# Routed rows without filled slots: shorter routing chunks in layer 1, and layer 3's expert groups that write finished tokens

## The chip, the cores and the metric

The kernel runs on one core of a Trainium2 chip. The metric is the device time of the whole program in microseconds; lower is better. Two engines matter most below beside TensorE (PE): VectorE (DVE), which does the small arithmetic of the routing, and GpSimd (POOL), which issues the indirect DMAs. ScalarE (ACT) evaluates functions, and SyncE (SP) issues ordinary DMAs.

## The reference, cut to what matters

Four transformer layers run one after another on 8192 tokens of width 128, in float32. Each layer is an attention (or scan) followed by a feed-forward part. The change concerns the feed-forward parts of layers 1 and 3, which are mixtures of 8 experts.

```python
# layer 1 (top 2 of 8, hidden width 512)
logits = xf @ gate_w + gate_b
top_w, top_i = jax.lax.top_k(logits, K)                 # K = 2
gw = jax.nn.softmax(top_w, axis=-1)
combine = (gw[:, :, None] * one_hot(top_i, E)).sum(axis=1)
for e in range(E):
    h = gelu(xf @ w1[e] + b1[e])
    out = out + combine[:, e:e + 1] * (h @ w2[e] + b2[e])
shared = gelu(xf @ ws1 + bs1) @ ws2 + bs2
return out + shared

# layer 3 (one expert of 8: the best of 4 groups, then the better of its 2; hidden width 256)
x = layernorm(x + attn_out, ln1_g, ln1_b)
combine = one_hot(flat_e, E) * (g_prob * e_prob)[:, None]
moe = sum over e of combine[:, e] * (relu(x @ w1[e] + b1[e]) @ w2[e] + b2[e])
x = layernorm(x + moe, ln2_g, ln2_b)
```

Around every part stands a residual of the form `x = x + part(layernorm(x))`. So the last output is layer 3's input plus its second layernorm.

## The kernel before, in words

**Tokens.** The 8192 tokens stand as 64 tiles of 128 (NT = 64). The residual `K.x` stays in on-chip memory for the whole program.

**Slots.** Class `Slots` sorts tokens by expert through DRAM. `rows` has room for 8 experts, each with 8192+256 slots. A row is the token's 128 numbers, the place to which its result goes, and its weight. `fill` writes all 67584 slots of each layer in advance with blanks: zeros, and a place that lies behind the tokens and differs for each slot. It runs on POOL beside layer 0's feed-forward part: an `iota` (L333) for the places and a DMA (L337) of 390 KB, 88 times a layer.

**Routing.** A chunk of 16 tiles is routed at once. `settle` closes the norms of a chunk (DVE). `gate` turns tokens and computes logits (PE, ACT, DVE). `choose` picks the experts and their weights. `places` counts tokens per expert with matmuls and a scan, and gives every token its slot. Then `send` casts the 128 slots of a tile to integers (`one`, L1422, a ring of 8 tiles) and issues an indirect DMA on POOL that writes 128 rows to their slots (L478). Layer 1 has two copies of each token; between them `second` rewrites the place (L373) and weight (L1417) of the chunk's rows, and it has to wait for the first copies' sends. In layer 1 these are generators, and `beside(n, most)` advances each by n steps and issues up to `most` sends after each step of the attention or of the shared feed-forward part. The order of PE, ACT and DVE is written out by hand in this way, so an instruction that waits holds everything behind it on its engine.

**Layer 1.** 16 attention steps overlapped in stages (four tiles each) are followed by the shared feed-forward part. Its expert work starts when all rows are sent. `S.finish` works out, for every group of 256 slots, its expert and its first slot.

**Groups.** `experts` walks over groups of 256 slots (72 in layer 1, 40 in layer 3: as many as full groups would need, plus one for each expert). `fetch` reads `xs` (SP, L513), copies the expert's weights `w` (L520) and second bias `b2` (L522) on DVE, casts `place` (L524), transposes on PE (L527) and copies `xT` on DVE (L529). `rise` multiplies by the first weight (PE, L538) and applies the function (ACT, L544). `fall` multiplies by the second (PE, L552 and L557), multiplies by the weight (DVE `y`, L563) and issues two indirect DMAs that write 128 results each to `back` (POOL, L484). `xs` and `y` have four buffers.

**After the groups.** Layer 1's results are read back by the next stage. Layer 3's tail reads eight tiles at a time (`join`, L2639), adds them to the rows `y`, takes the statistics, normalizes (ACT, L2648), multiplies by gamma (DVE, L2655), adds the residual (POOL, L2656) and writes to the output with SP. In layer 3 the rows of all 64 tiles stay in one tile of on-chip memory (`row`), and the space also serves the stage between layers 2 and 3 (`middle`) as scratch. Layer 3's expert weights `w_all` are loaded by 16 DMAs and one for the bias on SP, when the attention has ended (L2618 to L2623).

Of the kernel before, what the change touches and what calls it, by code (L numbers as in the profile page):

```python
# [20 lines left out]
P = 128  # L21
# [203 lines left out]
class Norm:  # L225
# [18 lines left out]
    def take(self, src, lo, hi):  # L244
        for j in range(lo, hi):
            self.nc.vector.bn_stats(self.st[:, j, :], src[:, j, :])  # L246
# [57 lines left out]
class Slots:  # L304
# [8 lines left out]
    GROUP, WIDE, NE = 256, D + 2, 8  # L313
    ROOM = NT * P + GROUP

    def __init__(self, K, es, tag, ranks):
        self.K, self.tag, self.ranks = K, tag, ranks
        self.groups = ranks * NT * P // self.GROUP + self.NE
        self.count = self.NE * self.ROOM
        dram = K.pool(es, tag + "slots", 1, DRAM)  # L320
        self.rows = dram.tile([self.count, self.WIDE], F32, name=f"{tag}_rows")
        self.back = dram.tile([self.count + ranks * NT * P, D], F32, name=f"{tag}_back")

    def fill(self, pool):
        nc = self.K.nc
        n = 6
        blank = [pool.tile([P, n, self.WIDE], F32, name=f"blank{i}") for i in range(2)]
        for t in blank:
            nc.gpsimd.memset(t, 0.0)
        rows = self.rows.rearrange("(c p n) w -> c p n w", p=P, n=n)  # L330
        for i in range(self.count // P // n):
            t = blank[i % 2]
            nc.gpsimd.iota(  # L333
                t[:, :, D], pattern=[[1, n]], base=i * n * P, channel_multiplier=n,
                allow_small_or_imprecise_dtypes=True,
            )
            nc.gpsimd.dma_start(rows[i], t)  # L337

    def begin(self, pool, most):

        nc = self.K.nc
        self.every = pool.tile([P, P], BF16, name="every")
# [6 lines left out]
        self.go_on = pool.tile([P, self.NE, most], F32, name="go_on")  # L349
        nc.gpsimd.memset(self.go_on, 1.0)  # L350
        nc.gpsimd.memset(self.go_on[:, :, 0:1], 0.0)
# [19 lines left out]
    def belongs(self, row, j, n, rank):  # L371

        self.K.nc.gpsimd.iota(  # L373
            row[:, j : j + n, D], pattern=[[P, n]], base=self.count + (rank * NT + j) * P,
            channel_multiplier=1, allow_small_or_imprecise_dtypes=True,
        )

    def places(self, pool, bank, picks, out):
# [4 lines left out]
        n, most = picks[0].shape[1], self.go_on.shape[2]  # L383
# [23 lines left out]
        if n == most:  # L407
            nc.vector.tensor_tensor_scan(
                sums.rearrange("p e n -> p (e n)"), self.go_on.rearrange("p e n -> p (e n)"),
                total.rearrange("p e n -> p (e n)"), 0.0, ALU.mult, ALU.add,  # L410
            )
        else:
            for e in range(NE):
                nc.vector.tensor_tensor_scan(
                    sums[:, e, :], self.go_on[:, e, 0:n], total[:, e, :], 0.0, ALU.mult, ALU.add
                )
# [17 lines left out]
    def finish(self, pool, long, expert, start):  # L434
# [16 lines left out]
        past = pool.tile([1, n, NE - 1], F32, name="past")  # L451
        nc.vector.tensor_tensor(
            past, self.number.unsqueeze(2).to_broadcast([1, n, NE - 1]),
            end[0:1, 0 : NE - 1].unsqueeze(1).to_broadcast([1, n, NE - 1]), ALU.is_ge,
# [3 lines left out]
        nc.vector.tensor_scalar(expert, which, float(long), None, ALU.mult)  # L458
# [3 lines left out]
            past, past, need[0:1, 0 : NE - 1].unsqueeze(1).to_broadcast([1, n, NE - 1])  # L462
# [20 lines left out]
    def result(self, place, row):  # L483
        i = self.K.nc.gpsimd.indirect_dma_start(  # L484
            self.back, bass.IndirectOffsetOnAxis(ap=place, axis=0), row, None
        )
        self.free(self.tag + "result", i.ins)

    def experts(self, w_all, expert, start, F, act):
# [9 lines left out]
        with ExitStack() as ps:  # L499
            gp = K.pool(ps, tag + "g", 4)  # L500
            wp = K.pool(ps, tag + "gw", 3)
# [5 lines left out]
            def fetch(g):  # L507
# [4 lines left out]
                xs = gp.tile([P, N, self.WIDE], F32, name="xs")  # L512
                nc.sync.dma_start(  # L513
                    xs, self.rows[bass.ds(at, self.GROUP)].rearrange("(n p) w -> p n w", p=P)
                )
                at = nc.vector.value_load(
# [6 lines left out]
                place = gp.tile([P, N], mybir.dt.uint32, name="place")  # L523
                nc.vector.tensor_copy(place, xs[:, :, D])  # L524
# [4 lines left out]
                nc.vector.tensor_copy(xT, t)  # L529
# [19 lines left out]
            def fall(g):  # L549
# [12 lines left out]
                y = gp.tile([P, N, D], F32, name="y")  # L562
                nc.vector.tensor_mul(y, o, xs[:, :, D + 1 : D + 2].to_broadcast([P, N, D]))  # L563
                for i in range(N):
                    self.result(place[:, i : i + 1], y[:, i, :])

            with K.tc.manual_schedule(
                engines={nc.tensor.engine, nc.scalar.engine, nc.vector.engine, nc.sync.engine}
            ):
                for g in range(-1, self.groups + 1):  # L570
# [4 lines left out]
                    if g > 0:  # L575
                        fall(g - 1)

    def results(self, pool, n, eight):

        back = self.back[self.count :].rearrange("(r j p) d -> r p j d", r=self.ranks, p=P)  # L580
# [331 lines left out]
def l0_ffn(K):  # L912
# [4 lines left out]
    with ExitStack() as es:  # L917
# [44 lines left out]
        for slots in (K.slots1, K.slots3):  # L962
            slots.fill(sp)
# [289 lines left out]
def layer1(K):  # L1253
# [4 lines left out]
    FC, CHUNK = F // P, 16  # L1258
# [13 lines left out]
    with ExitStack() as es:  # L1272
# [16 lines left out]
        S.begin(sp, CHUNK)  # L1289
# [28 lines left out]
        def settle(lo):  # L1318
            hi = lo + CHUNK
# [15 lines left out]
        def gate():  # L1335
# [19 lines left out]
            if old is not None:  # L1355
                lo, at = 4 * old // CHUNK * CHUNK, 4 * old % CHUNK
                if at == 0:
                    logits[lo] = lw.tile([P, CHUNK, NE], F32, name="lg")
# [4 lines left out]
                if at == CHUNK - 4:  # L1363
                    active.append((choose(lo), lo))
# [4 lines left out]
        def choose(lo):  # L1369
            n, hi = CHUNK, lo + CHUNK  # L1370
            lg = logits.pop(lo)

            def new(name, *shape):
                return rw.tile([P, n, *shape], F32, name=name)
# [30 lines left out]
            yield from S.places(rw, lambda: hold.pop(lo), picks, slots)  # L1405
            sum_e = new("sum_e")
            nc.vector.tensor_scalar_add(sum_e, e, 1.0)
            yield
            w0 = row[:, lo:hi, D + 1]
# [5 lines left out]
            def second():  # L1415
                S.belongs(row, lo, n, 1)
# [8 lines left out]
            S.belongs(row, lo, n, 0)  # L1425
# [39 lines left out]
        with ExitStack() as at:  # L1465
# [79 lines left out]
            def third(blk):  # L1545
# [21 lines left out]
                if (4 * blk + 4) % CHUNK == 0:  # L1567
                    active.append((settle(4 * blk + 4 - CHUNK), None))

            with K.tc.manual_schedule(  # L1570
# [3 lines left out]
                for n in range(NBLK + 5):  # L1574
# [3 lines left out]
                    beside(10, 5)  # L1578
# [5 lines left out]
        with ExitStack() as ps:  # L1584
# [30 lines left out]
            with K.tc.manual_schedule(  # L1615
                engines={nc.tensor.engine, nc.scalar.engine, nc.vector.engine}
            ):
                for n in range(NBLK + 1):
# [4 lines left out]
                    beside(14, 4)  # L1623
# [5 lines left out]
        S.experts(w_all, expert, start, F, AF.Gelu)  # L1629
# [13 lines left out]
def attention(K, es, tag, rows, wq, wk, wv, qb, kb, wo, bias, dst, causal, beside, done, more):  # L1643
# [124 lines left out]
    def turn(b):  # L1768
# [7 lines left out]
        if bias is not None:  # L1776
            y = dst[:, 2 * b : 2 * b + 2, :]
# [171 lines left out]
    def join(b):  # L1949
# [8 lines left out]
        def add():  # L1958
            y = dst[:, 2 * b : 2 * b + 2, :]
# [71 lines left out]
def l2_attn(K):  # L2031
    nc, ins = K.nc, K.ins
    DC = 32
    with ExitStack() as es:
# [66 lines left out]
        for _ in attention(  # L2101
            K, es, "a2", rows, w[:, 0, :], w[:, 1, :], w[:, 2, :], None, None, wo, None, K.x, True,
            beside, done, more,
# [5 lines left out]
def middle(K, scratch, fills):  # L2109
# [6 lines left out]
    with ExitStack() as es:  # L2116
# [46 lines left out]

        def xT(blk):
            return scratch[:, blk * 512 : (blk + 1) * 512]
# [183 lines left out]
def l3_ffn(K):  # L2349
# [7 lines left out]
    with ExitStack() as es:  # L2357
        sp = K.pool(es, "f3", 1)
        row = sp.tile([P, NT, S.WIDE], F32, name="y")
        y = row[:, :, 0:D]  # L2360
# [12 lines left out]
        with ExitStack() as ps:  # L2373
# [46 lines left out]
            def rows(b):  # L2420
                while ready[0] < 2 * b + 2:
                    next(entering, None)
                for j in (2 * b, 2 * b + 1):
                    nc.scalar.activation(
                        y[:, j, :], K.x[:, j, :], AF.Identity, bias=nmr[:, j : j + 1],
                        scale=first.r[:, j : j + 1],
                    )
                return y[:, 2 * b : 2 * b + 2, :]
# [5 lines left out]
            def settle(lo):  # L2434
# [5 lines left out]
                for j in range(lo, hi, 2):  # L2440
                    two = y[:, j : j + 2, :]
# [10 lines left out]
            def gate(bank, late):  # L2452
# [8 lines left out]
                if new is not None:  # L2461
                    for i in range(2):
                        nc.tensor.transpose(t[:, i * P : (i + 1) * P], y[:, new + i, :], K.ident)
# [315 lines left out]
```

## Time and profile before

| what | value |
|---|---|
| median of 3 runs | 3095.63 us (3092.87 to 3099.08) |
| profiled execution | 3072.12 us, its span 3070.4 us |
| TensorE clock granted, mean | 0.906 |
| PE, DVE, ACT, POOL busy | 81%, 60%, 46%, 28% of the span |
| layer 0 | 0 to 833 us |
| layer 1: attention, shared part, end of sends, groups | 855 to about 1000, 991 to 1123.5, to 1202.7, to 1485 |
| layer 2 and the middle | 1520 to 2260 us |
| layer 3: attention, last sends and weights, groups, tail | 2260 to 2850, to 2876.9, to 2996, to 3070.4 |

The stages are read from the windows of the profile, counted from the start of the span. A busy share is an average over stages with different limits. A stage's limit is read from its own window: which engine is busy there, and which wait ends last.

### The profile page before, as it was taken

Reading aid. Unit: us, or ns where it says so; the run is one execution under the profiler, and the core shown is the slowest. Engines: PE = TensorE matmul, PEld = TensorE weight load, DVE = VectorE, ACT = ScalarE, POOL = GpSimd, SP = SyncE. Lnnn points to the kernel's source line nnn. Section 1 sums busy time; section 2 is a strip of 40 time slices with the busy share of each in tenths; the row PEclk is TensorE's granted clock in tenths of the full one; section 3 lists DMA queues with packets and bytes.
Section 4 is the critical chain, followed back from the end, with each engine's and each line's share of the span. In section 5 each row is a group of like instructions: output and inputs, shape, how many; then the busy total and the mean of one; then the engine's idle time right before and its main releaser. Section 6 shows DMA issues by size and latency. Waiting matters only on the chain.

```text
span 3070.4 us, 59293 instructions
## 1 busy us (share of the span) xinstructions
PE 2481.3 (81%) x21486; PEld 1840.0 (60%) x21486; DVE 1853.4 (60%) x5498; ACT 1426.3 (46%) x3065; POOL 853.9 (28%) x1235
## 2 busy tenths in 40 slices
PE   4899787899889962999488888996978888887470
PEld 4865444444857742999466667775855555555460
DVE  7215454444878312444379766764869988886447
ACT  3433432222468521444435555556427677776223
POOL 1001444310012455455310101100520223343573
PEclk9999789999989986999779989997979999999795
DMA  2497455540000211222455434430034445451334
GB/s 72 141 283 223 173 231 228 217 152 21 12 1 13 82 40 52 70 70 70 117 155 160 128 113 141 132 95 13 1 86 137 128 125 143 130 147 42 91 91 112
DMA packets 263264, 340.81 MB, mean 111 GB/s; under 512 B 34598, under 2 KB 231062, under 8 KB 254780
## 3 DMA queue, kind: packets, MB, share of 16 engines
q1 hardware_dynamic: 231228, 237.01, 27.1%
q0 software_dynamic: 27584, 97.92, 8.5%
q8 instruction: 170, 2.79, 0.4%
q10 hardware_dynamic: 4160, 2.10, 0.3%
q14 instruction: 122, 1.00, 0.1%
HBM read 156.72 MB, written 177.83 MB: 109 GB/s over the span
## 4 chain that ended last, share of the span: by engine, by line
PE 39%; DVE 12%; DMA 7%; issue 5%; ACT 5%; POOL 4%; SPq 1%; DVEq 0%; POOLq 0%; ACTq 0%
PE o L1909 5%; PE t L1888 5%; DVE top L1845 4%; PE o L557 4%; PE hp L538 4%; DMA q<-row 4%; PE s L1784 2%; PE s L1833 2%; POOL f_back L484 2%; PE d L1607 2%; PE a L1592 2%; ACT e L1896 2%; DMA f_rows<-row,one 2%; DVE st_x L246 1%; PE a L1492 1%
## 5 line engine op out<-in xcount | busy, mean ns | idle before, releaser
L1845 DVE TENSOR_REDUCE top<-s 128x3 f32<-128x384 f32 (+1 forms) x1024 | 600.5, 617 | 189.5 <-PE s L1742 133.3
L1896 ACT ACTIVATE e<-t 128x384 f32<-128x384 f32 (+1 forms) x1024 | 494.0, 546 | 128.2 <-PE s L1742 82.7
L1888 PE MATMUL t<-q,k 64*128 64x256 f32 (+1 forms) x2048 | 417.1, 308 | 115.8 <-ACT e L1896 60.9
L1833 PE MATMUL s<-k,q 48*128 48x256 f32 (+1 forms) x2048 | 437.8, 331 | 30.3 <-DMA k<-d 16.7
L1888 PEld LDWEIGHTS t<-q,k 64*128 64x128 f32 x2048 | 299.7, 191 | 194.8 <-ACT e L1896 90.2
L1833 PEld LDWEIGHTS s<-k,q 48*128 48x128 f32 x2048 | 308.2, 198 | 43.6 <-DVE top L1845 23.9
L544 ACT ACTIVATE h<-hp,w 128x256 f32<-128x256 f32 x368 | 154.6, 471 | 332.8 <-PE hp L538 324.0
L484 POOL DMA_INDIRECT f_back<-y,place x224 | 217.4, 970 | 191.8 <-DVE y L563 125.8
L1909 PE MATMUL o<-e,val 128*32 128x256 f32 (+1 forms) x4096 | 262.0, 376 | 0.0
L538 PE MATMUL hp<-xT,w 128*128 128x256 f32 x736 | 184.4, 390 | 20.4 <-DVE xT L529 20.3
L557 PE MATMUL o<-w,h 128*128 128x128 f32 x1472 | 183.4, 276 | 0.0
L2079 POOL TENSOR_SCALAR xn<-x_sb,mean_x,r_x 128x128 f32<-128x128 f32 x64 | 55.2, 871 | 449.4 <-PE t L1773 394.0
L557 PEld LDWEIGHTS o<-w,h 128*128 128x128 f32 x1472 | 174.0, 193 | 1.5
L1909 PEld LDWEIGHTS o<-e,val 128*32 128x32 f32 x4096 | 110.7, 113 | 81.8 <-issue 12.8
L538 PEld LDWEIGHTS hp<-xT,w 128*128 128x128 f32 x736 | 133.4, 194 | 40.8 <-DVE xT L529 26.4
L1742 PE MATMUL s<-hideq,pick 64*128 64x128 bf16 x1024 | 151.6, 233 | 0.0
L478 POOL DMA_INDIRECT f_rows<-row,one x128 | 123.4, 964 | 94.2 <-DVE one L1422 61.7
L1742 PE MATMUL t<-hidek,pick 64*128 64x128 bf16 x1024 | 147.3, 227 | 0.0
L527 PE MATMUL t<-ident,xs 128*128 128x128 f32 x224 | 43.9, 278 | 101.4 <-DMA xs<-f_rows 101.4
L563 DVE TENSOR_TENSOR y<-o,xs 128x256 f32<-128x256 f32 x112 | 47.3, 422 | 114.2 <-PE o L557 113.9
L337 POOL DMA_DIRECT2D f_rows<-blank x176 | 98.3, 559 | 54.5 <-POOL blank L333 51.2
L775 PE MATMUL up<-wc,hT 128*128 128x128 f32 x768 | 110.8, 297 | 0.0
(522 smaller groups left out, 5294.8 us busy)
## 6 DMA issues: line engine op xcount, KB each, us to landing
f_rows<-blank POOLq DMA_DIRECT2D x176, 390.0 KB, 2.8
tz<-kpad SPq DMA_DIRECT2D x64, 512.0 KB
d<-high SPq DMA_DIRECT2D x128, 256.0 KB
d<-low SPq DMA_DIRECT2D x128, 256.0 KB
q<-d SPq DMA_DIRECT2D x128, 256.0 KB
k<-d SPq DMA_DIRECT2D x128, 256.0 KB
xs<-f_rows SPq DMA_DIRECT2D x112, 130.0 KB
t<-f_back SPq DMA_DIRECT2D x24, 512.0 KB
```

Of the source, the lines that this page charges most:

```text
L478: i = self.K.nc.gpsimd.indirect_dma_start(self.rows, bass.IndirectOffsetOnAxis(ap=slot, axis=0), row, None)
L484: i = self.K.nc.gpsimd.indirect_dma_start(self.back, bass.IndirectOffsetOnAxis(ap=place, axis=0), row, None)
L538: nc.tensor.matmul(hp[:, i, :], w[:, (c + i) * P : (c + i + 1) * P], xT, start=True, stop=True,)
L544: nc.scalar.activation(h[:, c + i, :], hp[:, i, :], act, bias=w[:, b1 : b1 + 1])
L557: nc.tensor.matmul(o[:, i, :], h[:, c, i * P : (i + 1) * P], w[:, F + c * D : F + c * D + D], start=False, stop=i == N - 1 and c == FC - 1,)
L775: nc.tensor.matmul(o, hT[:, 2 * blk + b, s : s + P], wc[:, j, cs], start=j == 0, stop=False)
L1742: nc.tensor.matmul(t.rearrange("p (n q) -> p n q", n=3)[:, 0:3:2, 64 * n : 64 * n + 64], pick[r, n, :], hide[name][r], start=False, stop=n ...
L1833: nc.tensor.matmul(s[:, lo:hi], q[r, p, h * P : (h + 1) * P], k[r, p, 0 : hi - lo], start=h == 0, stop=not causal and h == 1,)
L1845: nc.vector.tensor_reduce(tops[b][:, :, j, p], out_of["s"][:, 0:used].rearrange("q (h k) -> q h k", h=3 if causal else 2), axis=AX.X, op=A ...
L1888: nc.tensor.matmul(t[:, kh * SEQ : kh * SEQ + SEQ - skip], k[r, p, kh * P : (kh + 1) * P], q[r, p, skip:SEQ], start=kh == 0, stop=not caus ...
L1896: nc.scalar.activation(e, t, AF.Exp)
L1909: nc.tensor.matmul(o[32 * i : 32 * i + 32, skip:SEQ], val[b % RING][:, kh, 4 * m + i, 16 * s : 16 * s + 32], e[:, kh * SEQ : kh * SEQ + SE ...
```

## The change

It has five parts.

1. `fill` is gone. After the last chunk's `places`, eight blanks of 256 rows are written behind each expert's last token, and one at the very end of the slots at the start (`blanks`, `put_blank`, on SP's queue). The first `xs` waits for all of them. All blank rows have the same place, one past the last token, and `result` has a bounds check that drops them. `back` has room for tokens only.
2. There is one group fewer in each layer: 71 and 39.
3. Layer 1's chunks are 8, 8, 8, 8, 16 and 16 tiles. An attention step is followed by 18 instead of 10 steps of routing, a step of the shared part by 5 instead of 4 sends.
4. Layer 3's rows are twice as wide: the token after its first layernorm, and behind it the residual plus the second layernorm's beta. They stand in a ring of 18 pairs of tiles instead of one large tile. A gate comes at every second turn, and place and weight are written pair by pair.
5. Layer 3's tail is gone. Each group's `leave` multiplies by the weight and adds the token (`r`), takes the statistics, and for each four groups works out the norm; then `out_of` normalizes on ACT, multiplies by gamma on DVE, adds the second half of the row on POOL, and writes to the output itself by the indirect DMAs. This work lies between the steps of later groups (up to 11 units a group). `xT` is copied by ACT in layer 3, and `xs` and `place` have 12 buffers there.

The stage between layers 2 and 3 gets a scratch tile of its own.

```diff
-    def fill(self, pool):
...
-            nc.gpsimd.dma_start(rows[i], t)
...
+        self.groups = self.tokens // self.GROUP + self.NE - 1
...
+        nc.gpsimd.memset(self.blank[:, :, self.PLACE], float(self.tokens))
+        self.put = []
+        self.put_blank(self.count - self.GROUP)
...
+    def put_blank(self, at):
+        i = self.K.nc.sync.dma_start(
+            self.rows[bass.ds(at, self.GROUP)].rearrange("(n p) w -> p n w", p=P), self.blank
+        )
+        self.free(self.tag + "send", i.ins)
+        self.put.append(i.ins)
+
+    def blanks(self, pool):
+        nc = self.K.nc
+        last = pool.tile([1, self.NE], mybir.dt.int32, name="last")
+        nc.vector.tensor_copy(last, self.seen[0:1, :])
+        for e in range(self.NE):
+            self.put_blank(
+                nc.sync.value_load(
+                    last[0:1, e : e + 1], min_val=0, max_val=self.count - self.GROUP
+                )
+            )
...
         i = self.K.nc.gpsimd.indirect_dma_start(
-            self.back, bass.IndirectOffsetOnAxis(ap=place, axis=0), row, None
+            self.back, bass.IndirectOffsetOnAxis(ap=place, axis=0), row, None,
+            bounds_check=self.tokens - 1, oob_is_err=False,
         )
...
-                nc.vector.tensor_copy(xT, t)
+                copy(xT, t)
...
-                y = gp.tile([P, N, D], F32, name="y")
-                nc.vector.tensor_mul(y, o, xs[:, :, D + 1 : D + 2].to_broadcast([P, N, D]))
-                for i in range(N):
-                    self.result(place[:, i : i + 1], y[:, i, :])
+                leave(g, o, xs, place)
...
-    FC, CHUNK = F // P, 16
+    CHUNKS = [range(lo, lo + 8) for lo in (0, 8, 16, 24)] + [range(32, 48), range(48, NT)]
...
+            if hi == NT:
+                S.blanks(rw)
...
-                    beside(10, 5)
+                    beside(18, 5)
...
-                    beside(14, 4)
+                    beside(14, 5)
...
-                nc.vector.reciprocal(row[:, lo:hi, D + 1], low)
+                for j in range(lo, hi, 2):
+                    two = row_of[j // 2]
+                    nc.vector.reciprocal(two[:, :, S.WEIGHT], low[:, j - lo : j - lo + 2])
+                    S.belongs(two, j, 2, 0)
...
-                nc.gpsimd.tensor_add(two, two, spread(2, 3))
+                nc.gpsimd.tensor_add(
+                    row_of[b][:, :, D : 2 * D], K.x[:, 2 * b : 2 * b + 2, :], spread(2, 3)
+                )
...
-                if t % TURNS == 2 or t >= NB * TURNS:
+                if t % 2 == 0 or t >= NB * TURNS:
                     gate(bank, late)
...
+            BATCH, SETS = 4, 4
...
+            def out_of(g, j, r, xs, place):
+                for i in range(2):
+                    nc.scalar.activation(
+                        r[:, i, :], r[:, i, :], AF.Identity, bias=nmr[:, j + i : j + i + 1],
+                        scale=first.r[:, j + i : j + i + 1],
+                    )
+                nc.vector.tensor_mul(r, r, spread(2, 2))
+                nc.gpsimd.tensor_add(r, r, xs[:, :, D : 2 * D])
+                for i in range(2):
+                    S.result(place[:, i : i + 1], r[:, i, :])
...
+            def leave(g, o, xs, place):
+                if g is not None:
+                    j = g // BATCH % SETS * tiles + 2 * (g % BATCH)
+                    r = yp.tile([P, 2, D], F32, name="r")
+                    for i in range(2):
+                        nc.vector.scalar_tensor_tensor(
+                            r[:, i, :], o[:, i, :], xs[:, i, S.WEIGHT : S.WEIGHT + 1],
+                            xs[:, i, 0:D], ALU.mult, ALU.add,
+                        )
+                        nc.vector.bn_stats(first.st[:, j + i, :], r[:, i, :])
+                    batch.append((g, j, r, xs, place))
...
+            S.experts(w_all, expert, start, F, AF.Relu, leave, 3 * BATCH, nc.scalar.copy)
...
-            for q in range(5):
-                if q < 4:
-                    for i in (16 * q, 16 * q + 8):
-                        join(i)
-                    close(16 * q, 16 * q + 16)
-                if q:
-                    for i in range(16 * q - 16, 16 * q, 4):
-                        end(i)
```

## The prediction, made before the changed kernel ran

> **What bounds the kernel now.** I read the totals and the slices of the page first, then a table of windows cut at the stage borders, then the waits inside the windows where PE is idle.
>
> ```profile
> PE 2481.3 (81%) x21486; PEld 1840.0 (60%) x21486; DVE 1853.4 (60%) x5498; ACT 1426.3 (46%) x3065; POOL 853.9 (28%) x1235
> ...
> PE   4899787899889962999488888996978888887470
> ...
> POOL 1001444310012455455310101100520223343573
> ```
>
> PE carries the kernel, but its row falls to 2 in slice 15, to 4 in slice 37 and to 0 at the end. The change works on those three places. POOL's 4s in slices 4 to 6 are the fills of the slots. The windows give the price of each place (columns: window, length, then busy time and instructions of PE, PEld, DVE, ACT, POOL, then PE's granted clock, DMA share, GB/s):
>
> ```profile
> 1000.00:1060.00 60.00, 59.07 (x346) 43.51 (x346) 21.66 (x101) 31.36 (x55) 27.37 (x31) 0.96 0.29 88
> 1120.00:1160.00 40.00, 3.42 (x31) 3.23 (x29) 5.59 (x37) 0.00 (x0) 28.11 (x31) 0.60 0.15 47
> 1160.00:1203.00 43.00, 0.00 (x0) 0.00 (x0) 9.28 (x40) 0.00 (x0) 30.09 (x33) 0.50 0.15 50
> 1203.00:1485.00 282.00, 278.84 (x1941) 258.54 (x1942) 126.41 (x364) 122.17 (x290) 137.77 (x149) 0.99 0.24 68
> 2876.90:2996.00 119.10, 95.10 (x600) 81.53 (x600) 57.60 (x198) 33.60 (x80) 77.85 (x80) 0.96 0.32 88
> 2996.00:3070.40 74.40, 0.00 (x0) 0.00 (x0) 57.28 (x168) 25.06 (x64) 26.50 (x17) 0.50 0.41 114
> ```
>
> From 1123.5 (end of layer 1's shared FFN) to 1202.7 (first read of `xs`) only POOL works: it sends rows to their slots, 0.96 us each, one every 1.262 us. Then 72 groups run at PE's pace (278.84 of 282), 3.84 us each measured from `xs` to `xs`. In layer 3, 40 groups take 119 us; then 74 us have no PE at all: the results are read back, added, normalized, written. Who waits, from 1120 to 1203 and in layer 3's groups:
>
> ```profile
> DVE one L1422 <- DMA f_rows<-row,one: 60.4, 51, 3.3
> ```
>
> ```profile
> L484 POOL DMA_INDIRECT f_back<-y,place x80 | 78.5, 981 | 44.9 <-DVE y L563 23.7 <-issue 19.2 <-DVE b L522 1.4
> L520 DVE COPY w<-w_all 128x514 f32 x39 | 17.5, 449 | 12.1 <-DVE y L563 10.3 <-issue 0.7
> ```
>
> The first line: the index cast `one` waits for the send eight before it, so POOL and its DMA set the pace. The others: POOL is busy 78.5 of 119 us in layer 3's groups.
>
> **1. Layer 1's sends start earlier (-39.5 us).** Chunks of 16 tiles become 8, 8, 8, 8, 16, 16, with 18 steps of routing beside an attention step instead of 10, and 5 sends instead of 4 beside a shared step. In the order of instructions of both kernels, sends begin at attention step 12 instead of 19, and 38 casts `one` instead of 5 lie in steps up to 19. At 5 a step, 26 steps (12 to 37) take 130 of the 134 items (128 sends, 6 changes of a row for its second copy).
> The cost is on DVE, in order: steps 6 to 19 hold 217 small routing operations instead of 105. With my durations (0.21 us from start to start on up to 32 columns, 0.29 to 0.33 on 128x128) DVE's work there is 124.9 us instead of 98.2. These 14 steps take 108.9 us now, and DVE is busy 99.7 of 112 (880 to 992); those without routing take 6.8 us, those with it 8.7 to 10.8, so DVE's extra shows. I take +22 us (15 if PE's idle time absorbs some, 32 if waits for sends add to it). POOL has room: 5 sends are 6.3 us a step plus `q`'s add 1.38, in steps of about 9. One pair of activation table loads, 1.28 us each, goes from the shared stage (-2 us).
> So the shared FFN ends near 1123.5+22-2 = 1143.5. Then about 11.5 sends are left or under way, 14.5 us, and 2.5 us for a late change of a row (a wait for landing): 1160.5; landing 2.3 us: the first `xs` near 1163 instead of 1202.7.
>
> **2. One group fewer (-3.8 us in layer 1).** 71 instead of 72 at 3.84 us. Layer 3's is in part 5.
>
> **3. Fills go (0), blanks come (+4).** The fills are 176 DMAs of 0.56 us and 176 iotas of 0.14 us on POOL, 123 us, beside layer 0's FFN, where PE is busy 246.5 of 290 us (360 to 650): off the path, so 0. At most they give 8 us: ACT's `xn` waits 9.6 us there for a weight's load beside the fills' traffic, at the start. If PE has something else to wait for, nothing. Eight blanks a layer replace them: `value_load` and DMA on SP, each about 1.2 us like a group's `xs`, 9.6 us a layer, issued once `seen` of the last chunk is there. In layer 1 SP has nothing else then, and sends last longer: 0. In layer 3 they stand in SP's queue before 7 of the 16 loads of `w_all` and the bias; these end at 2863.6 now, and the copy of the bias, then `w`, then the first `xs` wait for them. Loads 11 us later meet the last sends (ending 2873.3): I take +4 (0 if sends still end last, 6 if loads do).
>
> **4. Layer 3's attention (+3).** The reciprocal split in 4 adds 3x8 small DVE operations, 24x0.2 = 4.8 us where DVE is busy 492 of 590 us; 32 iotas of 0.15 us on POOL (busy 170 of 590). Gates at every second turn, the same number in all. The `x` part is added to the row instead of in place: same POOL add. Sends carry 1032 bytes instead of 520; 64 of them, POOL's price is per row of a list (0.96), so I take 0 there. The ring of 18 pairs is reused after some 32 us, the sends long landed. I take +3 (0 to 8).
>
> **5. Layer 3's groups finish their tokens (-16.5).** DVE per group: gap for the register 0.42, `w`, `b2`, `place` 0.45+0.22+0.20, less 0.2 since neighbours overlap (57.6 us busy for 40 groups is 1.44 each, five durations sum to 1.70); two multiply-adds from PSUM 0.56 (0.28 each in layer 1's L1562); two statistics 0.41; multiply by gamma 0.42; 21 norm steps per four groups (20 take 3.76 us in the tail) 1.0; wait for ACT's normalization about 0.35: 3.8 us. `xT` goes to ACT (0.37), which then has about 2.1. PE 2.4. POOL: add of 128x256 0.7 and two results 2.52: 3.2.
> POOL's add beside DVE is the open cost. In the tail, the same pair of operations shows it:
>
> ```profile
> L2655 DVE TENSOR_TENSOR y<-y,b_f_ln x16: 683/1659/1670, 3021.3 to 3060.4; 128x512 f32<-128x512 f32 x16
> L2656 POOL TENSOR_TENSOR x_sb<-x_sb,y x16: 1172/1622/2164, 3022.1 to 3063.0; 128x512 f32<-128x512 f32 x16
> ```
>
> DVE's product is 0.68 us alone, 1.66 beside POOL's add (min, median, max in the row). At half the width that is +0.4 if they meet; I take +0.3. The Trainium skill ("GPSIMD Engine Reference", 8. Key points) says that POOL shares its interfaces with DVE, in contention with any DVE instruction on two SBUF inputs or in a two-port mode, and "Trainium Architecture — The Big Picture" (What this means for kernel authors) calls it an exclusive lock, not a split. By the rule each add could hold DVE for its whole 0.7 us, whichever of `w`, `b2` or the product it meets: 4.5 us a group, 16 us more in all, and the gain of this part is gone. By the row the product alone pays: 4.1. The row decides, since DVE's PSUM operations fill most of the group; the rule stays in the range.
> 39 groups at 4.1 are 160 us. Behind them: the last three groups' norm steps 4, first ACT and product 1.5, POOL 3x3.2, landing 2.3: 17. Together 177 against 193.5 (2876.9 to 3070.4). Bounds: 3.5 a group gives -40, 4.6 gives +3.
>
> **6. Results with a bounds check (0).** No row shows it. It can't be cheaper than nothing: same instruction, same list. Nearest row: 0.96 us without. Up to +0.66 each hides in layer 1 under PE's 3.84 per group (2x1.262 now), up to +0.44 in layer 3 under DVE's 4.1. I take 0 on the path; upper end +1 us each.
>
> **Sum.** -39.5-3.8+0+4+3-16.5 = -52.8 us against the profiled execution, 3072.1 to 3019. That execution is 23.5 us (0.8%) below the median of the three runs; I take the difference from the median: 3095.6-52.8 = 3043.
>
> **The rivals.**
> A, slower: the bounds check makes each result 1 us dearer. Layer 1's POOL then needs 4.52 per group, 0.68 over PE: 71x0.68 = 48 us. Layer 3's needs 5.2, 1.1 over DVE: 44 us, and 6 at the end. Total -52.8+98 = +45: 3140. It decides from about 0.8 us each. Against it: the list is 128 numbers and the whole of it takes 0.96 us now.
> B, larger gain: PE or idle time covers the routing (-22), the fills were felt (-8), and layer 3 runs at POOL's 3.4 (-27): up to -110, 2986. For it: PE is busy 107.6 of 112 us in that attention window. Against: routing steps are longer today.
> C, the lock holds DVE in layer 3 (4.6 a group): that stage gains nothing, 3060 to 3065.
> D, the change does not do what it says: casts in DVE's queue wait for sends during attention, so that 32 us or more are lost where sends are won; layer 1 then gains 15 and the total is -28: 3068.
>
> **How the numbers follow.** The forecast with parts mis-sized (3018 to 3068, with most of C): 0.74. B beyond that, below 3018: 0.10. D, or C with a second loss, above 3068 and still faster: 0.06. No change: 0.02. A or its like: 0.08. The range 3000 to 3082 leaves out A, no change, and the edge of B and D. A measurement tells apart about 0.2%, 6 us. Faster 0.90, same 0.02, slower 0.08.
>
> **What would show it.** First `xs` of layer 1 some 40 us earlier, with PE idle before it about 20 us instead of 79; attention steps 6 to 19 some 22 us longer; groups of layer 1 still at 3.84 and bound by PE; layer 3's groups at about 4.1 with DVE busiest; results at 0.96 us; about 17 us from PE's end to the program's. Results over 1.6 us, layer 3's groups over 4.6, or a first `xs` after 1185 would prove me wrong.

## The result, and the profile after

The changed kernel takes 3044.7 us (median of 4, 3040.2 to 3049.9) against 3094.3 us of the kernel before beside it (3083.9 to 3099.1): a ratio of 0.985, interval 0.982 to 0.988. Two later sets of runs, each with its own runs of the kernel before, gave 0.989 (0.985 to 0.992) and 0.993 (0.990 to 0.996). In microseconds of the medians these are 49.5, 33.6 and 24.0. It is faster each time, and the size varies by more than one set's interval.

The totals and rows of the changed kernel's page:

```profile
PE 2519.6 (83%) x21448; PEld 1867.8 (61%) x21448; DVE 1885.6 (62%) x5757; ACT 1431.7 (47%) x3112; POOL 739.9 (24%) x941
...
PE   4899788899978896999489999987978888887473
...
POOL 1001100000013554555211110001510234433366
```

The fills have gone from POOL's slices 4 to 7, and the last slices of PE are 4, 7, 3 instead of 4, 7, 0: the groups reach nearly to the end. The windows of the places that the prediction argued from (columns as before: window, length, busy time and count of PE, PEld, DVE, ACT, POOL, PE's clock, DMA share, GB/s):

```profile
1148.00:1178.00 30.00, 4.18 (x35) 3.77 (x32) 8.69 (x31) 1.95 (x3) 17.71 (x20) 0.65 0.12 40
1177.90:1460.00 282.10, 278.19 (x1917) 257.14 (x1917) 126.05 (x362) 121.38 (x289) 140.38 (x148) 0.98 0.23 65
...
2853.00:3015.00 162.00, 108.32 (x570) 91.80 (x569) 127.53 (x492) 67.88 (x184) 95.62 (x102) 0.84 0.28 77
3015.00:3040.20 25.20, 0.00 (x0) 0.00 (x0) 3.94 (x12) 2.42 (x6) 13.65 (x16) 0.50 0.05 14
```

PE works 4 of the 30 us before layer 1's first `xs`; before, it stood idle for 79. Layer 1's groups are bound by PE as they were. In layer 3's groups DVE is now the busiest engine (127.5 of 162), and PE waits.

The total hides where this comes from, so here is each stage in three profiles of the kernel before and three of the changed one. A stage runs from the start of one instruction to that of another, as the tile views list them; each cell has the profiles in the order `before`, `before_again`, `before_third` and `after`, `after_again`, `after_b`.

| stage (us) | before | changed | mean change |
|---|---|---|---|
| layer 1, first tanh to first `xs` | 345.3, 344.9, 345.2 | 322.1, 322.8, 314.0 | -25.5 |
| layer 1's groups, from there to the last `h` | 279.4, 279.7, 279.6 | 278.1, 277.8, 275.8 | -2.3 |
| layer 2's attention, first to last exponential | 525.6, 505.1, 515.2 | 506.4, 507.7, 500.5 | -10.4 |
| middle, to layer 3's first exponential | 210.5, 212.9, 211.3 | 213.7, 215.1, 214.8 | +3.0 |
| layer 3's attention, first to last exponential | 525.0, 519.4, 522.4 | 531.0, 535.0, 533.1 | +10.8 |
| to the last send | 50.2, 50.2, 50.4 | 45.0, 45.5, 43.3 | -5.7 |
| last send to first `xs` of layer 3 | 2.3, 2.3, 2.4 | 12.8, 13.9, 9.7 | +9.8 |
| first `xs` to PE's end | 116.7, 116.8, 118.7 | 167.4, 167.0, 166.3 | +49.5 |
| PE's end to the end | 79.1, 78.9, 78.9 | 29.8, 30.6, 30.3 | -48.7 |

The last two rows nearly cancel. Layer 3's new groups give nothing back; the gain that can be placed is layer 1's. Layer 2's attention differs between executions of one kernel by 20 us, which is as much as most parts of the change.

### The profile page after: what moved, and what is told of

The parts are those of the page before. It is cut to its first block, busy times and chain, and to the rows that moved or that the text cites. A ratio compares the mean times of both kernels' runs of the same rounds, so it can differ in the third digit from the quotient of the medians.

```text
span 3040.2 us, 59550 instructions
## 1 busy us (share of the span) xinstructions
PE 2519.6 (83%) x21448; PEld 1867.8 (61%) x21448; DVE 1885.6 (62%) x5757; ACT 1431.7 (47%) x3112; POOL 739.9 (24%) x941
## 4 chain that ended last, share of the span: by engine, by line
PE 38%; DVE 12%; issue 6%; DMA 5%; ACT 5%; POOL 3%; SPq 1%; another core or an unknown queue 0%; POOLq 0%; ACTq 0%; DVEq 0%
PE o L1954 5%; PE t L1933 5%; PE hp L565 4%; DVE top L1890 4%; PE o L584 4%; DMA q<-row 4%; PE s L1829 2%; PE s L1878 2%; POOL out L497 2%; ACT e L1941 2%; PE a L1624 1%; PE d L1639 1%; PE t L1787 1%; PE s L1973 1%; SPq L1922 1%
## 5 line engine op out<-in xcount | busy, mean ns | idle before, releaser
L1933 PE MATMUL t<-q,k 64*128 64x256 f32 (+1 forms) x2048 | 424.8, 310 | 95.0 <-ACT e L1941 45.8
L565 PE MATMUL hp<-xT,w 128*128 128x256 f32 x724 | 192.2, 407 | 51.2 <-DVE b L549 47.5
L491 POOL DMA_INDIRECT f_rows<-row,one x192 | 186.3, 970 | 156.5 <-ACT one L2620 53.5
L584 PE MATMUL o<-w,h 128*128 128x128 f32 x1448 | 189.5, 284 | 0.2 <-ACT h L571 0.2
L584 PEld LDWEIGHTS o<-w,h 128*128 128x128 f32 x1448 | 180.6, 201 | 2.8 <-ACT h L571 0.6
L565 PEld LDWEIGHTS hp<-xT,w 128*128 128x128 f32 x724 | 136.8, 202 | 73.9 <-issue 33.7
L497 POOL DMA_INDIRECT f_back<-y,place x142 | 140.8, 992 | 144.8 <-DVE y L1668 100.3
L547 DVE COPY w<-w_all 128x1028 f32 (+1 forms) x110 | 74.7, 679 | 67.4 <-DVE y L1668 28.9
L800 PEld LDWEIGHTS up<-wc,hT 128*128 128x128 f32 x768 | 103.5, 204 | 4.5 <-issue 2.8
L248 DVE BATCH_NORM_STATS2 st_x<-x_sb 128x6 f32<-128x128 f32 x448 | 101.3, 281 | 2.3
```

What stands on the lines that cost most here:

```text
L491: i = self.K.nc.gpsimd.indirect_dma_start(self.rows, bass.IndirectOffsetOnAxis(ap=slot, axis=0), row, None)
L497: i = self.K.nc.gpsimd.indirect_dma_start(self.back, bass.IndirectOffsetOnAxis(ap=place, axis=0), row, None, bounds_check=self.tokens - 1, ...
L565: nc.tensor.matmul(hp[:, i, :], w[:, (c + i) * P : (c + i + 1) * P], xT, start=True, stop=True,)
L584: nc.tensor.matmul(o[:, i, :], h[:, c, i * P : (i + 1) * P], w[:, F + c * D : F + c * D + D], start=False, stop=i == N - 1 and c == FC - 1,)
L800: nc.tensor.matmul(o, hT[:, 2 * blk + b, s : s + P], wc[:, j, cs], start=j == 0, stop=False)
L1933: nc.tensor.matmul(t[:, kh * SEQ : kh * SEQ + SEQ - skip], k[r, p, kh * P : (kh + 1) * P], q[r, p, skip:SEQ], start=kh == 0, stop=not caus ...
```

## The experiments

**What varies by itself.** The changed kernel ran twice more and the kernel before twice more, without an edit.

> The changed kernel once more, beside the three edits of it. Ratio to the kernel before about 0.985. Layer 2's attention, which the change hardly touches, took 20 us less in the profile of the changed kernel than in that of the kernel before. If that is the draw of one profiled execution, its length varies again here by some 10 to 20 us; if the change causes it (fewer fills, weights loaded earlier), it stays near 594 us.

> The kernel before once more, for its profile. If its 525 us in layer 2's attention were the draw of one execution, 505 to 530 are seen now; if they belong to the kernel, 520 to 530.

> The changed kernel once more, as the base for the next two on their chip. Ratio to the kernel before between 0.983 and 0.991; layer 2's attention from first to last exponential between 505 and 526 us, as a draw.

> The kernel before once more for its profile, on the chip of the three others. Layer 2's attention, 525.6 and 505.1 us in two profiles, shows a third draw; the stage from layer 1's attention to the first xs stays at 345 us, and the stage from layer 3's first xs to the end at 196.

Their profiles are in the table. The kernel before shows 525.6, 505.1 and 515.2 us in layer 2's attention, so the 19 us between the first two profiles need no effect of the change. They do not exclude a small one: the ten profiles of the changed kernel and its edits lie between 500 and 518 us, the four of the kernel before and of `l1_only` between 505 and 526. The other stages repeat within 6 us, apart from layer 1's in the changed kernel (322, 323, 314).

That stage differs with the set of runs, and not from one execution to the next. A set is what was timed together. The first comparison is one set; the second has `after_again`, `old_chunks`, `loads_act` and `no_add`; the third `l1_only`, `tiny_add`, `w_xt_on_act` and `before_again`; the fourth `after_b`, `w_on_act`, `fills_kept` and `before_third`. The last three ran on three different chips. With the same layer 1, the four profiles of the first two sets show 322.1 to 323.3 us, the five of the last two 310.6 to 314.0. In the longer ones DVE and ACT stand still for up to 11 us at a time in a wait that the profile calls remote (it found nothing on the core that ended it). The waits view of `after`, from 1020 to 1178:

```profile
DVE x_sb L1645 <- remote: 10.4, 1, 10.4
...
ACT h L1628 <- remote: 9.2, 1, 9.2
```

No profile of the last two sets, and none of the kernel before, has a remote wait above 1.5 us. What causes them is open. Within one set the layer-1 stage gained 23 us (first), 32 (third) and 31 (fourth). The ratios of `after_again` and `after_b` are those given above, and 0.993 lies a little outside what was expected.

**Layer 1's chunks: undone, and alone.** First the changed kernel with the old chunks:

```diff
-    CHUNKS = [range(lo, lo + 8) for lo in (0, 8, 16, 24)] + [range(32, 48), range(48, NT)]
+    CHUNKS = [range(lo, lo + 16) for lo in (0, 16, 32, 48)]
...
-                    beside(18, 5)
+                    beside(10, 5)
...
-                    beside(14, 5)
+                    beside(14, 4)
```

> The changed kernel with layer 1's chunks as before (4 of 16 tiles, 10 steps and 4 sends). Theory (the sends that come earlier are worth what the first read of xs shows): slower than the changed kernel by 22 to 28 us, first xs near 1200 us, attention of layer 1 some 21 us shorter. Rival (the routing in the attention costs as much as it gives): within 8 us of the changed kernel.

3079.6 us against 3056.8 of the changed kernel in the same set (ratios to the kernel before 0.996, 0.995 to 0.998, and 0.989): 22.8 us slower, as the theory had it. Its first `xs` comes at 1208.0, 356.5 us after the first tanh, 33.7 later than in `after_again`. The kernel before needs 345 in the profiles of the other sets; none was taken in this one, so whether those 11 us belong to the rest of the change or to this set is open.

Then the kernel before with the new chunks and nothing else:

```diff
-    FC, CHUNK = F // P, 16
+    FC = F // P
+    CHUNKS = [range(lo, lo + 8) for lo in (0, 8, 16, 24)] + [range(32, 48), range(48, NT)]
...
-                    beside(10, 5)
+                    beside(18, 5)
...
-                    beside(14, 4)
+                    beside(14, 5)
```

> The kernel before with layer 1's shorter chunks alone (8, 8, 8, 8, 16, 16; 18 steps, 5 sends); fills, 72 and 40 groups and the tail stay. Theory (this part gives what the first read of xs shows, and groups are bound by PE as before): first xs near 1178 us, faster than the kernel before by 22 to 28 us. Layer 2's attention tells about its 20 us: near 525 us from its first to its last exponential, as in the kernel before, if fills or the load order made the change; near 507 if the profile of the kernel before was an odd draw.

3029.6 us against 3054.7: 25.1 us faster, 0.991 (0.988 to 0.994). The stage to the first `xs` is 307.6 us, so it gained 37.5 us, more than expected and close to the prediction's 39.5. The tile view of `one` shows the sends (min, median, max in ns, then first and last start):

```profile
L474 POOL DMA_INDIRECT f_rows<-row,one x128: 952/963/1077, 946.7 to 1161.9; - x128
```

In the same set the whole change reached 312.9 and 312.8 us in this stage (`tiny_add`, `w_xt_on_act`), so the rest of it costs 5 us there. In both pairs the timed total moved by 11 to 12 us less than the stage (22.8 against 33.7, 25.1 against 37.5); where that goes was not followed. Layer 2's attention took 524.6 us here, with the fills and the load order of the kernel before. By itself that would have spoken for an effect of the change; `before_again`, with 505.1 in the same set and with the same fills and load order, shows that such a length can be a draw.

**The fills.** The changed kernel got the 176 fills back, into a scratch tensor of their own:

```diff
...
+        for _ in range(2):
+            rows = junk.rearrange("(c p n) w -> c p n w", p=P, n=6)
+            for i in range(88):
+                t = blank_j[i % 2]
+                nc.gpsimd.iota(
+                    t[:, :, D], pattern=[[1, 6]], base=i * 6 * P, channel_multiplier=6,
+                    allow_small_or_imprecise_dtypes=True,
+                )
+                nc.gpsimd.dma_start(rows[i], t)
```

> The changed kernel with the 176 fills of the kernel before put back beside layer 0's feed-forward part, into a scratch of their own. Theory (they are hidden there): within 3 us of the changed kernel, layer 0's feed-forward stage at most 2 us longer. Rival (their 69 MB take DMA from the weights' loads at the stage's start or slow layer 1): 5 to 10 us slower.

3036.7 us against 3038.5 without them: no difference that this set can tell (each ratio has an interval of 8 to 9 us to either side). The window of layer 0's feed-forward part, of the changed kernel and of this one:

```profile
360.00:650.00 290.00, 246.50 (x845) 129.26 (x844) 133.76 (x262) 86.05 (x151) 0.34 (x4) 0.95 0.03 7
```

```profile
360.00:650.00 290.00, 246.32 (x849) 130.76 (x850) 132.89 (x261) 86.38 (x151) 113.81 (x331) 0.95 0.60 232
```

POOL works 113 us more and DMA moves 232 instead of 7 GB/s, and PE does the same 246 us of work in the 290. Layer 1's first tanh, before which all of layer 0 lies, starts at 857.8 us, against 851.4 to 857.4 in the nine profiles of the changed kernel and its edits without fills. The 70 MB cost nothing that these profiles can tell from the draw of an execution.

**Layer 3's late start.** The chain of waits of the changed kernel there (start, length, what) runs through SP's queue:

```profile
2829.04 0.69 SPq L377
2829.74 0.69 SPq L377
...
2833.43 0.37 SPq L377
2833.85 0.27 SPq L390
...
2837.30 0.47 SPq L2680
...
2839.34 2.68 DMA w_all<-in_f_w
2842.15 0.29 SPq L526
2842.98 2.73 DMA xs<-f_rows
```

L390 and L377 are the blanks, L2680 a load of `w_all`. The blanks stand in the queue from 2820.2 to 2837.3, 2.1 us each in this profile instead of the 1.2 that I had assumed, seven loads and the bias come behind them, and the last send starts at 2830.2. So the loads were moved to ACT's queue:

```diff
-                nc.sync.dma_start(w_all[:, e, 0:F], ins["f3_w1"][e])
+                nc.scalar.dma_start(w_all[:, e, 0:F], ins["f3_w1"][e])
```

(and the other two load statements in the same way)

> The changed kernel with layer 3's expert weights loaded by ACT's queue instead of SP's, so that the eight blanks do not stand among them. Theory (the blanks hold the loads back and those hold the first xs): first xs of layer 3 right behind the last send's landing, 8 to 11 us earlier, the whole as much faster. Rival (sends or the count of groups end as late): less than 3 us.

3046.7 us against 3056.8, with overlapping intervals (0.983 to 0.989 and 0.985 to 0.992). The stage itself says that the theory was wrong: last send to first `xs` is 11.6 us instead of 13.9. `w` is ready at 2834.8 now, and still the first `xs` is issued at 2844.0, behind the blanks:

```profile
L491 POOL DMA_INDIRECT f_rows<-row,one x14: 959/963/975, 2814.8 to 2832.4; - x14
L377 SPq MOVE f_rows<-blank x8: 4/29/29, 2824.1 to 2841.3; - x8
L377 SPq DMA_DIRECT2D f_rows<-blank x8: 9/372/717, 2824.2 to 2841.4; - x8
```

Eight blanks take from 2822.4 to 2841.8, 2.4 us each, although nothing stands between them. In both kernels the first three or four are slow and the last ones take 1.15 us. I put the slow ones down to the loads in flight beside them (0.77 DMA share, 255 GB/s from 2820 to 2826 in the changed kernel). The later profiles speak against that. In `after_b`, with the same loads before and behind them, the blanks are quick:

```profile
L377 SPq DMA_DIRECT2D f_rows<-blank x8: 372/372/405, 2805.3 to 2814.8; - x8
```

Eight take 10.5 to 10.9 us in all five profiles of the last two sets, and 17 to 19 in all five of the first two. So the slow blanks go with the set, like layer 1's remote waits, and their cause is open as well. With blanks of 1.3 us the first `xs` still comes 9.0 to 9.7 us after the last send, about 7 later than in the kernel before: it stands in SP's queue behind eight blanks, seven loads and the bias. No run loads `w_all` earlier.

**What bounds layer 3's groups.** First the addition on POOL was left out:

```diff
-                nc.gpsimd.tensor_add(r, r, xs[:, :, D : 2 * D])
```

> The changed kernel without POOL's addition of the residual (and of beta) in layer 3's groups: that part of the computation is left out. Theory (the add holds DVE's two-input and copy operations, w, b2, place and the product): a group of layer 3 falls from 4.18 to 3.6 to 3.8 us, and the drain behind the last group by 7 x 0.65 us; in all 18 to 25 us faster. Rival (DVE's own work is the 4.18 us): the groups stay within 0.1 us, only the drain gains, about 5 us in all.

3073.5 us: 17 us slower. A group took 4.84 us from `r` to `r` instead of 4.13. The waits view names a new one, eight times in DVE's queue and about 5 us at most each time:

```profile
DVE r L2722 <- remote: 38.9, 8, 5.1
...
ACT h L571 <- remote: 16.6, 3, 6.3
...
ACT xT L556 <- remote: 12.0, 6, 2.7
```

In the stretch that I followed it ends when POOL has sent, or landed, the batch's last result; once for each batch of four groups. The profile does not name what was waited for, and this set shows remote waits in layer 1 too, so the edit answers neither theory. The next one keeps an instruction of POOL's in that place and only makes it short:

```diff
-                nc.gpsimd.tensor_add(r, r, xs[:, :, D : 2 * D])
+                nc.gpsimd.tensor_add(r[:, :, 0:4], r[:, :, 0:4], xs[:, :, D : D + 4])
```

> The changed kernel with POOL's addition in layer 3's groups on 4 of 128 columns: the residual is left out of the others. Unlike the run without the addition, POOL keeps an instruction between product and result, so that the waits stay as they are. Theory (POOL's add holds DVE's copies and the product for 0.42 us a group): 3.75 us a group instead of 4.2, 16 us, and some 4 us less in the drain: 20 us faster than the changed kernel. Rival (that time is filled by another wait): 5 us or less. If it is slower, as without the addition, the add itself was not what counted there.

3022.9 us against 3054.7 of the kernel before: 0.988 (0.984 to 0.993); the changed kernel was not in this set. The group falls from 4.14 to 3.83 us, and PE's end comes 155.6 us after the first `xs` instead of 167. With the way from there to the end (27.9 us instead of 30) that is 14 of the 20 us that were expected. The 5-us waits do not come; but no profile of this set has remote waits, so whether the instruction kept in place or the other chip removed them is open. The period of the changed kernel itself does not depend on the set (4.14, 4.13 and 4.13 us in its three profiles). The groups of instructions show where the time was (count, busy us, mean ns of one, idle time before). The changed kernel:

```profile
L2702 POOL TENSOR_TENSOR r<-r,xs 128x256 f32<-128x256 f32 x34 | 25.7, 769 | 69.1 <-DVE r L2701 69.1
L547 DVE COPY w<-w_all 128x514 f32 x36 | 23.4, 649 | 13.9 <-issue 13.4 <-ACT h L571 0.5
...
L2701 DVE TENSOR_TENSOR r<-r,b_f_ln 128x256 f32<-128x256 f32 x36 | 18.2, 543 | 9.5 <-ACT r L2697 9.5
...
L549 DVE CAST b<-w_all 128x128 bf16 x36 | 11.7, 325 | 0.0
L551 DVE CAST place<-xs 128x2 uint32<-128x2 f32 x36 | 8.5, 235 | 0.0
```

With the short addition:

```profile
L547 DVE COPY w<-w_all 128x514 f32 x36 | 16.1, 446 | 16.7 <-issue 16.7
...
L2701 DVE TENSOR_TENSOR r<-r,b_f_ln 128x256 f32<-128x256 f32 x36 | 14.4, 419 | 10.0 <-ACT r L2697 9.5
...
L549 DVE CAST b<-w_all 128x128 bf16 x36 | 8.0, 222 | 0.0
L2702 POOL TENSOR_TENSOR r<-r,xs 128x8 f32<-128x8 f32 x35 | 7.7, 232 | 69.1 <-DVE r L2701 69.1
L551 DVE CAST place<-xs 128x2 uint32<-128x2 f32 x36 | 6.3, 175 | 0.0
```

`w` loses 0.20 us, the product 0.12, `b2` 0.10, `place` 0.06: beside POOL's addition, copies are longer as well as the product. `no_add` confirms the first three (0.46, 0.42 and 0.22 us without any addition); `place` took 0.22 there, so its 0.06 may have another cause. A group gets shorter by 0.31 us.

Then `w` and `b2` went to ACT, with the register that picks the expert. As run, the edit holds for layer 3 alone (the expectation says both layers):

```diff
-                at = nc.vector.value_load(
+                at = eng.value_load(
...
-                nc.vector.tensor_copy(w, flat[:, bass.ds(at, REST)])
+                move(w, flat[:, bass.ds(at, REST)])
...
-                nc.vector.tensor_copy(b2, flat[:, REST:][:, bass.ds(at, D)])
+                move(b2, flat[:, REST:][:, bass.ds(at, D)])
```

with `eng, move = nc.scalar, nc.scalar.copy` in layer 3. Once `xT` stayed on ACT (`w_xt_on_act`), once it went back to DVE (`w_on_act`):

> The changed kernel with the copies of w and b2 (and the register load for them) on ACT instead of DVE, in both layers. Theory (DVE bounds layer 3's groups): DVE falls to about 3.1 us a group, ACT rises to about 3.2, POOL needs 3.3 to 3.9: groups of 3.5 to 3.9, 12 to 26 us faster than the changed kernel; layer 1 stays at 3.84. Rival (ACT becomes the chain, since h waits behind the copies): 4.2 us or more, no gain.

> The changed kernel with layer 3's copies of w and b2 and the register load for them on ACT, and xT's copy back on DVE. With xT on ACT too a group fell from 4.14 to 3.83 us with ACT at about 3.7 as the next chain. Theory (work is now spread evenly: DVE 3.5, ACT 3.4, POOL 3.3 to 3.9): 3.6 to 3.8 us a group, 13 to 20 us faster than the changed kernel. Rival (POOL's add and two results are the chain, at 3.8 or more): no better than with xT on ACT, 10 to 12 us.

3016.8 us, 0.987 (0.984 to 0.991), and 3029.3 us, 0.990 (0.987 to 0.993); the changed kernel beside the second gave 3038.5, 0.993 (0.990 to 0.996), so the intervals overlap. The groups fell to 3.83 and 3.79 us, and PE's end came 156.2 and 154.4 us after the first `xs`: 10 and 12 us less than 166 to 167. So DVE's copies were on the path. Both groups lie at the upper end of what was expected (3.5 to 3.9, then 3.6 to 3.8), and the gain of 10 to 12 us is what the rival of the second run had named. In the first one ACT is the new wait:

```profile
PEld hp L567 <- ACT xT L558: 52.1, 35, 3.9
PE hp L567 <- ACT xT L558: 45.3, 35, 3.7
```

Why moving `xT` away from ACT gave only 0.04 us more is open: POOL's addition and two results, at 3.27 us a group in the drain of the changed kernel, lie below both.

## Why the prediction was right, and where it was not

The forecast of 3043 us, 52.8 less, met the first comparison (49.5 less). The other two, 33.6 and 24.0, lie inside its range (14 to 96 less) but show that its centre was too low. That the first total came within 4 us is luck: parts 1 and 5 were to bring 56 us and show 25 in the stages, and parts 3 and 4 cost 18 instead of 7. The timed totals gained more than these stages explain. Part by part:

1. **Sends: -39.5 forecast, -25.5 measured.** The mechanism holds: the new chunks alone gave -37.5. What was mis-sized is the price of the routing on the way: the shared part was to end 20 us later (22 less 2) and ends 25 us later in `l1_only`, 28 in `after_b` and 31 in `after` (its last product starts 265.6 us after the first tanh before the change, then 290.6, 293.2 and 296.2). From there to the first `xs` I had 19.5 us; it takes 17.1, 20.8 and 25.9, with 12, 14 and 16 sends still to start where I had 11.5. In `after` POOL stands still from 1144.7 to 1150.7 there, because the sends are tied to PE's steps through `one` in DVE's order, and DVE stood in the remote wait shown above until 1147. The rest of the change costs 5 us in this stage in the one set that has both. The blanks are not shown to be the cause: SP has issued the last of them in layer 1 at 1097.9, 80 us before the first `xs`.
2. **One group fewer: -3.8, measured -2.3.** The period is 3.84 us in all. In two of the three profiles of the changed kernel the first two groups took 4.7 and about 5 us; in the third, without this, the stage is 3.8 us shorter.
3. **Fills: 0, shown** by `fills_kept`. **Blanks in layer 3: +4, measured +9.8.** The path was right, SP's queue with the loads behind the blanks, and the term mis-sized: with blanks of 1.3 us it is 7 us (third and fourth set), with 2.1 us it is 10.5 (first set).
4. **Layer 3's attention: +3, measured +8.1** with the middle and the way to the last send (3.0+10.8-5.7). In windows of the same stage DVE is busy 501.8 us in 600 against 492.1 in 590; the rest of the 10.8 us was not followed.
5. **Layer 3's groups and end: -16.5, measured +0.8.** This is the step that failed. The period was right (4.1 forecast, 4.14 measured). So was the size of POOL's hold on DVE (0.3 forecast, 0.31 measured), but by luck: I had put all of it on the product, which paid 0.12, and the copies paid the larger part. The ends were wrong. From the first transpose to the first `r` it took 8.2 us where one period was counted. Behind the last group I counted 17 us; from its `r` at 3011.4 to the end it is 28.8. POOL had seven groups before it at 3008.5, not three, since a batch's results are issued while later groups run; the last of 78 results starts at 3030.4. And from that result's end the program needs 8.8 us more (5.9 in `fills_kept`), where I counted 2.3 for the landing. The 4 us at the start and the 12 at the end are nearly all of the 17 us that are missing.
6. **Bounds check: 0, confirmed.** The groups of results in layer 1, of the kernel before and of the changed one:

```profile
L484 POOL DMA_INDIRECT f_back<-y,place x141 | 136.0, 965 | 146.0 <-DVE y L563 102.1 <-issue 36.6 <-DVE place L524 6.5
```

```profile
L497 POOL DMA_INDIRECT f_back<-y,place x140 | 138.8, 992 | 144.2 <-DVE y L1668 100.3 <-issue 39.8 <-DVE place L551 3.4
```

965 to 992 ns: 0.03 us each, far from the 0.8 at which rival A would have decided.

Rival C was the nearest in outcome, though by another way: layer 3's stage gained nothing, not because the lock made groups of 4.6 us, but because fill, drain and the program's end took what the period left. The rule of the Trainium skill ("GPSIMD Engine Reference", 8. Key points) that I weighed against the row was right in kind: copies get longer too, not the product alone. The price was 0.31 us a group, and not the whole 0.7.

The profiles that show stages add up to -21 us on average, of which 10.4 are layer 2's draw, and the timed medians to -36. That gap is within what layer 2's attention varies, but it was not resolved.

## What to carry to other kernels

A loop's period times its count is the easy part of such a sum. Count the fill of its pipeline, the backlog of its slowest queue at the end, and what the program needs after its last instruction; here these took a gain of 17 us, with the period right to 1%. And when two stages change in one edit, run one alone: here layer 1's chunks carried nearly all that could be placed. Compare a stage only with runs of its own set: layer 1's stage was 9 us longer, and eight blanks 7 us, in two sets than in the other two.

## What the runs showed of the hardware

- A bounds check on an indirect DMA of 128 rows cost 0.03 us of POOL's time (0.965 to 0.992).
- POOL's 0.7-us addition lengthened DVE's copies (0.45 to 0.65 us for 128x514) as well as its two-input product (0.42 to 0.54).
- 70 MB of writes by POOL's DMAs beside PE-bound work changed that work by nothing measurable (PE busy 246.3 and 246.5 us of 290).
- Eight writes on SP's queue, each with a register load, took 10.5 to 10.9 us in five profiles and 17 to 19 in five others of nearly the same kernel. The two groups are different sets of runs; the cause is open.
- An execution of layer 2's attention takes 500 to 526 us without an edit that bears on it. A stage has to be read in several profiles before 10 us of it are explained.
